# Attention scores in wider visits: from 20 steps of four PSUM banks to 12 visits of six

## The chip, the cores and the metric

The kernel runs on one core of one Trainium2 chip. A core has a matrix engine (TensorE; PE in the profile, PEld for its weight loads), a vector engine (VectorE; DVE), an activation engine (ScalarE; ACT), GpSimd (POOL) and a queue that starts transfers (SyncE; SP). Matrix products land in PSUM, which has eight banks of 512 float32 columns by 128 partitions; everything else works in SBUF. The metric is the device time of one execution in microseconds (us), the median of three runs, lower is better.

## The reference, cut to what matters

32 images of 256 channels by 1024 positions (S) pass a group norm, three 1x1 projections to queries, keys and values, and strictly causal attention with 8 heads of 32 channels; the input is added to the result. All is float32.

```python
q = einsum('oc,bcs->bos', q_w, gn(x)) + q_b          # and kv likewise; 8 heads of 32
mask = tril(ones((S, S)), -1)                        # key strictly before query
scores = where(mask == 0, -10000, q @ k^T / sqrt(32))
attn = where(mask == 0, 0, softmax(scores))
x = x + attn @ v
```

The kernel computes the exponentials without subtracting a maximum, sums them, and multiplies the result by the inverse sums. A slower path that subtracts the maximum stands behind a range check of the sums and isn't entered here.

## The kernel before, in words

**Tiling.** Scores are held transposed: 128 keys on the partitions, queries along the columns. A head has 32 channels, so a product of one head's keys and queries uses 32 of the 128 rows of the matrix array, and four heads (one of two groups `g`) are multiplied side by side, each on its own quarter of the rows and into its own PSUM bank. The queries of an image come in two halves `hf` of 512 columns; keys come in eight blocks `k` of 128. Blocks wholly hidden by the mask are not computed, and the short ends are packed: half 0 takes three steps, half 1 seven. Per image that is 2 x (3 + 7) = 20 steps, 12 of them 512 columns a head, 4 of them 384 + 128 columns (two key blocks in one step), 4 of them 256 columns.

**A step** (`scores`, line 243) takes two PSUM tiles of two banks each out of a pool of three (`ps_s`, six banks), multiplies the four heads into them (line 252; tile `sT` in the profile), lets ACT take the exponential of each tile into SBUF (line 259; tile `e`), and has POOL zero the masked corner (line 265). Two steps later (`LAG = 2`) `values` (line 273) multiplies those exponentials with the values of the four heads, side by side on four quarters of the array's columns, into one bank (`acc`, line 283), and DVE adds the exponentials into the running sum (line 288). Behind the last step of a half ACT copies `acc` out (`num`, line 292). `sums` (line 295) adds over the keys with a product of ones (`pd`, line 301), copied out by ACT (`den`, line 306).

**The projections** of the next image fill in between: twelve units per image, eight of 512 columns (`pp`, tiles `q` and `k`) and four for the values (`ppv`, tile `v`), each one bank of products (line 146) and one ACT copy (line 208 or 224). They, `pd` and the norm's tiny products (`pm`, `pv`) share one PSUM bank, `misc`. Six banks of `ps_s`, one of `acc` and one of `misc` make all eight.

**The order** on PE, ACT, DVE and POOL is written out by hand: at step `i` the scores of step `i`, then the functions entered for `i` in the table `at` (projections, norm, finishing), then the values of step `i - 2`, then the table `after` (the sums). The offsets are in `PROJECT`, `PREPARE`, `SUMS` and `FINISH` (lines 387 to 390). Each engine works through its list in order and waits for semaphores that the framework sets. The finished sums go through DRAM: SP writes `den` out, `gather` reads all four back as one tile, DVE inverts it, SP writes the inverse and reads it back spread over the partitions (`rb`), and DVE multiplies, adds the bias and `x` (`finish`, lines 346 and 347).

Of the kernel before, what the change touches and what calls it, by code (L numbers as in the profile page):

```python
# [17 lines left out]
P = 128  # L18
HD = 32
# [6 lines left out]
SUM_MAX = 1.0e20  # L26
ROW = 64
LAG = 2
# [3 lines left out]
def tile_norm_attention_residual(  # L32
# [83 lines left out]
    def unshifted():  # L116
        live = {}
        xpool = tc.alloc_tile_pool(name="xpool", bufs=4)
# [10 lines left out]
        qkpool = tc.alloc_tile_pool(name="qkpool", bufs=4)  # L129
        epool = tc.alloc_tile_pool(name="epool", bufs=4)  # L130
# [104 lines left out]
        def blocks(hf, k):  # L235

            d = k - hf * BPH
            own = slice(max(d, 0) * P, HALF)
            if d == 1:
                return [(k, own, own), (k + 2, slice(0, P), slice(HALF - P, HALF))]  # L240
            return [(k, own, own)]

        def scores(b, g, hf, k):
            q, kk = live["q", b, g], live["k", b, g]
            d = k - hf * BPH
            tag = "e0" if k == 0 else "e"
            e = epool.tile([P, 4, HALF], F32, tag=tag, bufs=3 if k == 0 else None, name=f"{tag}_{b}_{g}_{hf}_{k}")
            pairs = [ps_s.tile([P, 2, HALF], F32, tag="sT", name=f"sT_{b}_{g}_{hf}_{k}_{a}") for a in range(2)]
            for kb, cols, of in blocks(hf, k):
                for j in range(4):  # L250
                    rows = slice(HD * j, HD * (j + 1))
                    nc.tensor.matmul(  # L252
                        pairs[j // 2][:, j % 2, cols], lhsT=kk[rows, kb * P : (kb + 1) * P],
                        rhs=q[rows, hf * HALF + of.start : hf * HALF + of.stop],
                        start=True, stop=True, skip_group_check=True,
                    )
            c0 = 2 * P if d == 2 else 0
            for a in range(2):
                nc.scalar.activation(e[:, 2 * a : 2 * a + 2, c0:], pairs[a][:, :, c0:], AF.Exp)  # L259
            if d >= 0:  # L260


                n = 2 if d == 1 else 1
                diagonal = e[:, :, c0 : c0 + n * P].rearrange("p j (n q) -> p j n q", q=P)
                nc.gpsimd.affine_select(  # L265
                    out=diagonal, in_=diagonal, pattern=[[0, 4], [0, n], [1, P]],
                    compare_op=ALU.is_gt, fill=0.0, base=0, channel_multiplier=-1,
                )
                if k == 0:
                    nc.gpsimd.memset(e[0:1, :, 0:1], 1.0)  # L270
            live["e", b, g, hf, k] = e

        def values(b, g, hf, k):
            last = k == hf * BPH + 2
            e = live.pop(("e", b, g, hf, k))
            if k == 0:
# [3 lines left out]
            for kb, cols, of in blocks(hf, k):  # L280
                for j in range(4):
                    h = 4 * g + j
                    nc.tensor.matmul(  # L283
                        acc[HD * j : HD * (j + 1), of], lhsT=live["v", b][:, kb, h * HD : (h + 1) * HD],
                        rhs=e[:, j, cols], start=k == 0, stop=last, skip_group_check=True,
                    )
                if k:
                    nc.vector.tensor_add(total[:, :, of], total[:, :, of], e[:, :, cols])  # L288
            if last:
                if (g, hf) == (0, 0):  # L290
                    live["num", b] = work.tile([P, NG, S], F32, tag="num", name=f"num_{b}")
                nc.scalar.copy(live["num", b][:, g, hf * HALF : (hf + 1) * HALF], acc)  # L292
# [72 lines left out]
        per = [(g, hf, k) for g in range(NG) for hf in range(NH) for k in range(hf * BPH + 3)]  # L365
        steps = [(b, *s) for b in range(B) for s in per]
        N = len(per)
# [5 lines left out]
        def prepare(b, whens):  # L373
            both = [slice(hf * HALF, (hf + 1) * HALF) for hf in range(NH)]
            for n, f in zip(whens, (
# [4 lines left out]
                if n is None:  # L380
                    f()
                else:
                    when(n, f)
# [3 lines left out]
        PROJECT = (-6, -5, -3, -2, -1, 1, 4, 5, 7, 8, 9, 11)  # L387
        PREPARE = (-36, -35, -30, -28, -20, -19, -18, -18)
        SUMS = LAG + 2
        FINISH = (N + 11, N + 12, N + 14, N + 15)  # L390
        every = range(4)

        with tc.manual_schedule(engines={ENG.PE, ENG.Activation, ENG.DVE, ENG.Pool}):
            prepare(0, [None] * 8)
            for n, f in zip((None, None, 0, 0, 1, 1) + PROJECT[6:], projections(0)):
                if n is None:
                    f()
                else:
                    when(n, f)
            if B > 1:  # L400
                prepare(1, (None, None, 2, 4, 6, 7, 8, 9))
            for b in range(B):
# [4 lines left out]
                if b >= 2:  # L407
                    when(max(first - 2 * N - 2, 0), lambda b=b: load(b))
                    prepare(b, [first + n for n in PREPARE])
                for s, (g, hf, k) in enumerate(per):  # L410
                    if k == hf * BPH + 2:
                        n = first + s + (LAG if last and s == N - 1 else SUMS)
                        when(n, lambda b=b, g=g, hf=hf: sums(b, g, hf), after)
                if not last:
                    when(first + N + 4, lambda b=b: gather(b, every))
                    when(first + N + 6, lambda b=b: check_sums(b, every))
                    when(first + N + 6, lambda b=b: invert(b, every))
                    for n in every:
                        when(first + FINISH[n], lambda b=b, n=n: finish(b, n))
                else:  # L420
                    when(first + N - 4, lambda b=b: gather(b, every[:3]), after)
                    when(first + N - 2, lambda b=b: check_sums(b, every[:3]))
                    when(first + N - 2, lambda b=b: invert(b, every[:3]))
                    for n in every[:3]:
                        when(first + N + n - 1, lambda b=b, n=n: finish(b, n))
                    when(first + N + LAG, lambda b=b: gather(b, every[3:]))
                    when(first + N + LAG, lambda b=b: finish_last(b))
                    when(first + N + LAG, lambda b=b: check_sums(b, every[3:]))
            for i in range(max(max(at), max(after), len(steps) + LAG) + 1):
                if i < len(steps):  # L430
                    scores(*steps[i])
                for f in at.get(i, ()):
                    f()
                if LAG <= i < len(steps) + LAG:
                    values(*steps[i - LAG])
                for f in after.get(i, ()):
                    f()

# [6 lines left out]
        for p in reversed(pools):  # L445
            p.release()
        return outside
# [149 lines left out]
```

## Time and profile before

| | us |
|---|---|
| median of three runs | 2073.38 (2070.18 to 2073.43) |
| the profiled execution's own time | 2069.36 |
| its span in the trace | 2067.4 |
| PE busy | 2009.1 (97%) |
| ACT busy | 1501.4 (73%) |
| DVE busy | 1474.5 (71%) |
| POOL busy | 449.8 (22%) |

The granted TensorE clock is 0.994 of full speed over the span. A row of the profile names the line of the kernel, the engine, the operation, the tile written and those read, and the shape; a product in float32 leaves two MATMUL records, since the engine goes over it in two passes. The ends of MATMUL records are modelled, so the distance from one row's start to the next row's start says more than the length of a row.

### The profile page before, as it was taken

To read this page: it belongs to the slowest core of one execution; us is meant where nothing else is said; L and a number is where in the kernel's file an instruction comes from. 1 tells how busy PE (TensorE), PEld (TensorE's weight loads), DVE (VectorE), ACT (ScalarE), POOL (GpSimd) and SP (SyncE) were. 2 spreads that over 40 slices of the span, in tenths; PEclk is the share of its full clock that TensorE was granted. 3 is DMA by queue.
4 is the path that set the end of the run, shared out by engine and by line. 5 is a ranking of instruction groups with operands and counts; after the bars stand their busy time and mean duration, and the time that the engine had idled before them with its cause. 6 is when DMAs were issued, how large, how long until landed. Compare 5 with 4: busy or idle time off the path is not lost.

```text
span 2067.4 us, 50451 instructions
## 1 busy us (share of the span) xinstructions
PE 2009.1 (97%) x22030; PEld 712.0 (34%) x22030; DVE 1474.5 (71%) x1480; ACT 1501.4 (73%) x1991; POOL 449.8 (22%) x495
## 2 busy tenths in 40 slices
PE   7999999999999999999999999999999999999994
PEld 2333333333333333333333333333333333333331
DVE  3677777677777777776777777777767777777666
ACT  4777777777777777777777777777777777777773
POOL 1321221212212212212122122122122121222221
PEclk9999999999999999999999999999999999999997
DMA  2011011111111110111111111111111101111101
GB/s 100 2 64 64 34 54 44 63 64 45 50 48 52 63 65 33 55 46 61 64 56 42 48 50 64 64 36 52 49 58 65 64 34 51 47 64 44 39 34 54
DMA packets 56782, 107.76 MB, mean 52 GB/s; under 512 B 14188, under 2 KB 15340, under 8 KB 56556
## 3 DMA queue, kind: packets, MB, share of 16 engines
q1 hardware_dynamic: 54780, 103.56, 14.2%
q8 instruction: 174, 2.85, 0.6%
q10 hardware_dynamic: 1776, 0.92, 0.2%
q14 instruction: 52, 0.43, 0.1%
HBM read 68.82 MB, written 35.64 MB: 51 GB/s over the span
## 4 chain that ended last, share of the span: by engine, by line
PE 87%; ACT 4%; issue 4%; POOL 3%; DVE 1%; DMA 1%; ACTq 0%; POOLq 0%; SPq 0%; DVEq 0%
PE sT L252 27%; PE pp L146 23%; PE acc L283 23%; PE ppv L146 9%; PE pd L301 5%; POOL e L265 3%; ACT e L259 2%; ACT num L292 1%; ACT k L208 1%; DMA qk_bias<-in_L_conv_q_b_dram 0%; PE pm L146 0%; DVE e L288 0%; DMA rb<-inverses 0%; DVE rb L359 0%; DVE rb L347 0%
## 5 line engine op out<-in xcount | busy, mean ns | idle before, releaser
L259 ACT ACTIVATE e<-sT 128x1024 f32<-128x1024 f32 (+1 forms) x1280 | 1132.5, 937 | 461.1 <-PE sT L252 454.2
L288 DVE TENSOR_TENSOR e<-e,e 128x2048 f32<-128x2048 f32 (+3 forms) x640 | 1086.1, 1697 | 377.3 <-PE acc L283 258.7
L265 POOL TENSOR_SCALAR_AFFINE_SELECT e<-e 128x512 f32<-128x512 f32 (+1 forms) x384 | 420.5, 1095 | 1575.5 <-ACT e L259 1465.1
L252 PE MATMUL sT<-q,k 32*128 32x512 f32 (+3 forms) x6144 | 684.0, 524 | 0.8 <-ACT k L208 0.8
L283 PE MATMUL acc<-e,v 128*32 128x512 f32 (+3 forms) x6144 | 617.4, 489 | 18.8 <-ACT num L292 10.0
L146 PE MATMUL pp<-xn,wT 128*32 128x512 f32 x4096 | 493.7, 600 | 2.4 <-ACT q L208 0.9
L252 PEld LDWEIGHTS sT<-q,k 32*128 32x128 f32 x6144 | 273.1, 183 | 458.9 <-issue 384.0
L283 PEld LDWEIGHTS acc<-e,v 128*32 128x32 f32 x6144 | 175.1, 110 | 366.3 <-issue 232.8
L146 PE MATMUL ppv<-wT,xn 128*32 128x256 f32 x4096 | 247.6, 382 | 0.8 <-ACT k L208 0.8
L146 PEld LDWEIGHTS pp<-xn,wT 128*32 128x32 f32 x4096 | 107.1, 109 | 282.6 <-issue 174.1
L191 DVE TENSOR_SCALAR xn<-x,mean,rstd 128x512 f32<-128x512 f32 x128 | 73.0, 630 | 175.1 <-POOL rstd L184 175.1
L146 PEld LDWEIGHTS ppv<-wT,xn 128*32 128x32 f32 x4096 | 120.0, 109 | 123.8 <-ACT den L306 47.0
L301 PE MATMUL pd<-e,pick 128*32 128x512 f32 x1024 | 134.2, 596 | 13.3 <-DVE e L288 12.2
L208 ACT ACTIVATE q<-pp,qk_bias 128x512 f32<-128x512 f32 x128 | 88.1, 689 | 31.5 <-PE pp L146 31.5
L208 ACT ACTIVATE k<-pp,qk_bias 128x512 f32<-128x512 f32 x128 | 88.1, 688 | 28.7 <-PE pp L146 26.9
L347 DVE SCALAR_TENSOR_TENSOR rb<-rb,v_bias_col,x 128x512 f32<-128x512 f32 x129 | 105.6, 819 | 4.6
L346 DVE TENSOR_TENSOR rb<-num,rb 128x512 f32<-128x512 f32 x129 | 87.6, 679 | 4.3 <-DMA rb<-inverses 4.3
L306 ACT COPY den<-pd 128x512 f32<-128x512 f32 x128 | 75.0, 586 | 14.7 <-PE pd L301 14.7
L156 DVE BATCH_NORM_STATS2 st<-x 128x6 f32<-128x512 f32 x128 | 81.9, 681 | 5.2 <-DMA x<-in_x_dram 5.2
L224 ACT COPY v<-ppv 128x512 f32<-128x512 f32 x128 | 75.1, 586 | 4.2 <-PE ppv L146 2.1
L292 ACT COPY num<-acc 128x512 f32<-128x512 f32 x128 | 74.8, 585 | 3.9 <-PE acc L283 3.9
L301 PEld LDWEIGHTS pd<-e,pick 128*32 128x32 f32 x1024 | 31.8, 110 | 52.4 <-issue 37.7
(40 smaller groups left out, 153.5 us busy)
## 6 DMA issues: line engine op xcount, KB each, us to landing
x<-in_x_dram SPq DMA_DIRECT2D x64, 512.0 KB
rb<-inverses SPq DMA_DIRECT2D x127, 256.0 KB
out_dram<-rb SPq DMA_DIRECT2D x127, 256.0 KB
sums<-den SPq DMA_DIRECT2D x128, 8.0 KB
rows<-sums SPq DMA_DIRECT2D x31, 32.0 KB
inverses<-inv SPq DMA_DIRECT2D x31, 32.0 KB
wn<-in_L_conv_kv_w_dram ACTq DMA_DIRECT2D x2, 256.0 KB
wn<-in_L_conv_q_w_dram ACTq DMA_DIRECT2D x1, 256.0 KB
```

Of the source, the lines that this page charges most:

```text
L146: nc.tensor.matmul(out[part], lhsT=lhsT[:, part], rhs=rhs, start=start, stop=stop, skip_group_check=True)
L156: nc.vector.bn_stats(st[:, c, :], live["x", b][:, g, c * HALF : (c + 1) * HALF])
L208: nc.scalar.activation(live[key][:, cols], pp, AF.Identity, bias=qk_bias[:, n, g : g + 1], scale=(SCALE, 1.0)[n],)
L252: nc.tensor.matmul(pairs[j // 2][:, j % 2, cols], lhsT=kk[rows, kb * P : (kb + 1) * P], rhs=q[rows, hf * HALF + of.start : hf * HALF + of. ...
L259: nc.scalar.activation(e[:, 2 * a : 2 * a + 2, c0:], pairs[a][:, :, c0:], AF.Exp)
L265: nc.gpsimd.affine_select(out=diagonal, in_=diagonal, pattern=[[0, 4], [0, n], [1, P]], compare_op=ALU.is_gt, fill=0.0, base=0, channel_mu ...
L283: nc.tensor.matmul(acc[HD * j : HD * (j + 1), of], lhsT=live["v", b][:, kb, h * HD : (h + 1) * HD], rhs=e[:, j, cols], start=k == 0, stop= ...
L288: nc.vector.tensor_add(total[:, :, of], total[:, :, of], e[:, :, cols])
L292: nc.scalar.copy(live["num", b][:, g, hf * HALF : (hf + 1) * HALF], acc)
L301: nc.tensor.matmul(pd[HD * j : HD * (j + 1), :], lhsT=pick, rhs=total[:, j, :], start=True, stop=True, skip_group_check=True,)
L346: nc.vector.tensor_mul(rb[:, g, cols], num[:, g, cols], rb[:, g, cols])
L347: nc.vector.scalar_tensor_tensor(rb[:, g, cols], rb[:, g, cols], v_bias_col[:, g : g + 1], xt[:, g, cols], ALU.add, ALU.add)
```

## The change

A **visit** takes the place of a step. It holds a full piece (up to 512 columns for each of the four heads, in four banks) and a half piece (256 columns for each head, in two banks), and takes all three tiles of `ps_s` at once: six banks. There are 6 visits for a group of heads, 12 for an image. To have as many half pieces as full ones, key blocks 1 and 2 of half 1 are cut into two pieces of 256 columns each; the two 256-column ends of before are the other two half pieces. Columns in total stay as they were.

The half piece has four heads and two banks. Heads 2 and 3 are multiplied first, into the upper halves of banks 4 and 5; then the full piece, heads 0 to 3 into banks 0 to 3; then heads 0 and 1 into the lower halves of banks 4 and 5. The first two products raise a semaphore of their own (`bank_free`), on which TensorE waits before the last two. ACT takes three exponentials of 1024 elements (line 302 twice, line 303), where it took two.

The values lag by one visit, not two steps. The projections stand one at each visit. `values` of a half-cut block are two products of 256 columns with two additions on DVE. The tables of offsets are rewritten, and `prepare` and `finish` go into `after`, behind the values of their visit. Pools shrink: `qkpool` 4 to 3, `epool` 4 to 3, with a tag `eh` of 4 half-wide buffers. At the end of the last image the three first finishes stand behind all additions on DVE, and not between them.

On PE, before, in the second half of an image's first group of heads (`sT_0_1_3` are the scores of group 0, half 1, key block 3; `pp_1_0_0` is a projection unit; `pd_0` the first sum):

```order
L252 MATMUL sT_0_1_2_0_2144<-q_0_1830,k_0_1859 128x512 x2
L252 MATMUL sT_0_1_2_1_2145<-q_0_1830,k_0_1859 128x512 x2
L146 MATMUL pp_1_0_0_2153<-xn_1477,wT 32x512 x8
L283 MATMUL acc_0_1_2167<-e_3_0_1_0_2075,v_1907 32x512 x4
L252 MATMUL sT_0_1_3_0_2173<-q_0_1830,k_0_1859 128x512 x2
L252 MATMUL sT_0_1_3_1_2174<-q_0_1830,k_0_1859 128x512 x2
L283 MATMUL acc_0_1_2167<-e_0_1_1_2102,v_1907 32x512 x4
L301 MATMUL pd_0_2197<-e_3_0_0_0_1988,pick 32x512 x4
```

And now, the visit of the same key block:

```order
L255 MATMUL sT_0_1_3_2_2285<-q_0_1944,k_0_1988 128x256 x2
L255 MATMUL sT_0_1_3_0_2283<-q_0_1944,k_0_1988 128x512 x2
L255 MATMUL sT_0_1_3_1_2284<-q_0_1944,k_0_1988 128x512 x2
L255 MATMUL sT_0_1_3_2_2285<-q_0_1944,k_0_1988 128x256 x2
L147 MATMUL pp_1_0_0_2299<-xn_1590,wT 32x512 x8
L325 MATMUL acc_0_1_2309<-e_3_0_1_0_2227,v_2043 32x512 x4
L325 MATMUL acc_0_1_2309<-eh_0_0_1_2165,v_2043 32x256 x4
L325 MATMUL acc_0_1_2309<-eh_0_1_0_2228,v_2043 32x256 x4
L343 MATMUL pd_0_2324<-e_3_0_0_0_2118,pick 32x512 x4
```

Two runs of scores with values behind each have become one run of scores, one of projections, and one of values with the sum behind it.

On PE around the second unit of the value projection (`ppv_1`, key blocks 2 and 3), before; the values that read it first are those of `e_0_0_2`, three steps later and out of this piece:

```order
L146 MATMUL ppv_1_854<-wT,xn_509 32x256 x16
L283 MATMUL acc_1_1_694<-e_1_1_6_787,v_731 32x256 x4
L252 MATMUL sT_0_0_2_0_880<-q_0_657,k_0_683 128x256 x2
L252 MATMUL sT_0_0_2_1_881<-q_0_657,k_0_683 128x256 x2
L283 MATMUL acc_0_0_894<-e_1_0_0_0_812,v_731 32x512 x4
```

And now; `eh_0_0_0` holds key block 2, which needs `ppv_1`:

```order
L255 MATMUL sT_0_0_1_2_2168<-q_0_1944,k_0_1988 128x256 x2
L147 MATMUL ppv_1_2186<-wT,xn_1590 32x256 x16
L325 MATMUL acc_0_0_2204<-e_3_0_0_0_2118,v_2043 32x512 x4
L325 MATMUL acc_0_0_2204<-eh_0_0_0_2119,v_2043 32x256 x4
L343 MATMUL pd_3_2214<-e_2_1_1_0_1927,pick 32x512 x4
```

The products that read that projection have come to stand one product behind it.

On ACT, before (`den_0` is the copy of `pd_0`):

```order
L259 ACTIVATE e_0_1_2_1555<-sT_0_1_2_0_1556 128x1024
L259 ACTIVATE e_0_1_2_1555<-sT_0_1_2_1_1557 128x1024
L208 ACTIVATE q_1_1564<-pp_1_0_0_1565,qk_bias 128x512
L259 ACTIVATE e_0_1_3_1584<-sT_0_1_3_0_1585 128x1024
L259 ACTIVATE e_0_1_3_1584<-sT_0_1_3_1_1586 128x1024
L306 COPY den_0_1614<-pd_0_1609 128x512
```

And now:

```order
L302 ACTIVATE e_0_1_3_1649<-sT_0_1_3_0_1651 128x1024
L302 ACTIVATE e_0_1_3_1649<-sT_0_1_3_1_1652 128x1024
L303 ACTIVATE eh_0_1_3_1650<-sT_0_1_3_2_1653 128x2x2x256
L209 ACTIVATE q_1_1666<-pp_1_0_0_1667,qk_bias 128x512
L348 COPY den_0_1697<-pd_0_1692 128x512
```

The copy of a projection stands behind three exponentials of its visit, not two. The diff, cut to its core:

```diff
-        qkpool = tc.alloc_tile_pool(name="qkpool", bufs=4)
-        epool = tc.alloc_tile_pool(name="epool", bufs=4)
+        qkpool = tc.alloc_tile_pool(name="qkpool", bufs=3)
+        epool = tc.alloc_tile_pool(name="epool", bufs=3)
...
+        def scores(b, full, half):
...
+            e = epool.tile([P, 4, HALF], F32, tag=tag, name=f"{tag}_{name}")
+            eh = epool.tile([P, 4, HALFBANK], F32, tag="eh", bufs=4, name=f"eh_{name}")
+            pairs = [ps_s.tile([P, 2, HALF], F32, tag="sT", name=f"sT_{name}_{a}") for a in range(3)]
+            short = pairs[2].rearrange("p bank (n q) -> p bank n q", n=2)
+            first = [scores_of((b, half), short[:, j % 2, 1, :], j, name) for j in (2, 3)]
+            for j in range(4):
+                scores_of((b, full), pairs[j // 2][:, j % 2, :], j, name)
+
+            for ins in first:
+                ins.then_inc(bank_free, 1)
...
+            live["free"] = live.get("free", 0) + len(first)
+            wait = nc.tensor.wait_ge(bank_free, live["free"])
...
+            for j in range(2):
+                lo = scores_of((b, half), short[:, j, 0, :], j, name)
...
+            for a in range(2):
+                nc.scalar.activation(e[:, 2 * a : 2 * a + 2, :], pairs[a], AF.Exp)
+            exp = nc.scalar.activation(eh.rearrange("p (n bank) q -> p bank n q", n=2), short, AF.Exp)
...
+            mask(full, e)
+            mask(half, eh)
...
+            visits += [
+                (f[0][0], f[0][2]), (f[0][1], h[1, 0]), (f[1][0], h[1, 1]),
+                (f[1][3], h[2, 0]), (f[1][4], h[2, 1]), (f[1][5], f[1][6]),
+            ]
+            products += [
+                (f[0][0], f[0][2]), (f[0][1],), (f[1][0], h[1, 0], h[1, 1]),
+                (f[1][3], h[2, 0]), (f[1][4], h[2, 1]), (f[1][5], f[1][6]),
+            ]
...
-        PROJECT = (-6, -5, -3, -2, -1, 1, 4, 5, 7, 8, 9, 11)
-        PREPARE = (-36, -35, -30, -28, -20, -19, -18, -18)
-        SUMS = LAG + 2
-        FINISH = (N + 11, N + 12, N + 14, N + 15)
+        PROJECT = (-4, -3, -2, -1, 0, 1, 2, 3, 4, 5, 6, 7)
+        PREPARE = (-22, -21, -20, -19, -18, -16, -11, -11)
+        SUMS = (3, 7, 9, 13)
+        FINISH = (N + 7, N + 7, N + 8, N + 9)
...
-            for i in range(max(max(at), max(after), len(steps) + LAG) + 1):
-                if i < len(steps):
-                    scores(*steps[i])
-                for f in at.get(i, ()):
+            for i in range(B * N + 1):
+                if i < B * N:
+                    scores(i // N, *visits[i % N])
+                for f in at.pop(i, ()):
                     f()
-                if LAG <= i < len(steps) + LAG:
-                    values(*steps[i - LAG])
-                for f in after.get(i, ()):
+                if i:
+                    for pc in products[(i - 1) % N]:
+                        values((i - 1) // N, pc)
+                for f in after.pop(i, ()):
                     f()
```

In `visits` and `products`, `f[hf][k]` is the full piece of key block `k`, and `h[k, n]` the n-th 256 columns of a cut block.

More of the change, by code (lines that the diff above doesn't have):

```diff
@@ L230, in projections, with piece @@
             return qk[0] + v[:1] + qk[1] + v[1:3] + qk[2] + v[3:] + qk[3]
-        def blocks(hf, k):
+        def piece(g, hf, k, part=None):
             d = k - hf * BPH
-            own = slice(max(d, 0) * P, HALF)
             if d == 1:
[L240 to L257, printed above, removed]
-            for a in range(2):
[L259 to L271, printed above, removed]
@@ L426, in unshifted @@
[L426 to L436 removed]
+                        when(first + N, lambda b=b, n=n: finish(b, n), after)
@@ L446, in unshifted @@
             p.release()
+        for ins in nc.cur_bb.bb.instructions:
+            if "TilePoolBoundary op=release" in ins.concise():
+                tc.declare_no_dep(ins, group="first", reason="exponentials behind them are waited for")
         return outside
```

104 lines of the change are left out of this document (77 added, 27 removed).

## The prediction

> **What bounds the kernel now.** First the page: span, busy time and the chain that ended last.
>
> ```profile
> span 2067.4 us, 50451 instructions
> PE 2009.1 (97%) x22030; PEld 712.0 (34%) x22030; DVE 1474.5 (71%) x1480; ACT 1501.4 (73%) x1991; POOL 449.8 (22%) x495
> PE 87%; ACT 4%; issue 4%; POOL 3%; DVE 1%; DMA 1%; ACTq 0%; POOLq 0%; SPq 0%; DVEq 0%
> ```
>
> TensorE sets the end, so the question is what its time is made of. The chain in order of time shows the same product once an image:
>
> ```profile
> 124.99 1.90 PE pp L146 x16
> ...
> 1763.68 1.90 PE pp L146 x16
> ```
>
> These lie 26 images apart: 1638.69 / 26 = 63.03 us an image. 32 images are 2017; the other 50 us are head and tail. Next, PE's own rows in the middle of an image; I read distances from start to start.
>
> ```profile
> 1020.68 1.04 PE L283 MATMUL acc<-e,v 128*32 128x512 f32 x8
> 1021.65 1.14 PE L252 MATMUL sT<-q,k 32*128 32x512 f32 x8
> 1022.72 1.06 PE L283 MATMUL acc<-e,v 128*32 128x512 f32 x8
> 1023.61 1.04 PE L301 MATMUL pd<-e,pick 128*32 128x512 f32 x8
> 1024.58 1.14 PE L252 MATMUL sT<-q,k 32*128 32x512 f32 x8
> 1025.65 1.93 PE L146 MATMUL ppv<-wT,xn 128*32 128x256 f32 x32
> 1027.40 1.04 PE L283 MATMUL acc<-e,v 128*32 128x512 f32 x8
> 1028.37 1.15 PE L252 MATMUL sT<-q,k 32*128 32x384 f32 x16
> 1029.45 1.92 PE L146 MATMUL pp<-xn,wT 128*32 128x512 f32 x16
> 1031.19 1.04 PE L283 MATMUL acc<-e,v 128*32 128x512 f32 x8
> 1032.16 0.71 PE L252 MATMUL sT<-q,k 32*128 32x256 f32 x8
> 1032.81 1.50 PE L146 MATMUL pp<-xn,wT 128*32 128x512 f32 x12
> ```
>
> Scores of 512 columns take 1.07 (1024.58 to 1025.65), of 256 columns 0.65: 0.42 for 256 columns, both passes, four heads abreast. `pp` runs 1024 columns in 1.74, at most 0.00170 a column. I use 0.00167, 0.43 per 256. What is left is fixed: 1.07 - 0.85 = **0.22** for going into scores and out again, whatever their width (0.65 - 0.43 is 0.22 too). Values of 512 columns take 0.89 with `pd` behind them and 0.97 with scores behind them (both 0.85 by columns), so the way into scores adds 0.12. Every run of scores costs **0.34** beyond its columns, 20 times an image, 6.8 of 63.
>
> **The change, part by part.**
>
> *Fewer runs of scores.* 12 instead of 20: 8 x 0.34 = -2.72 an image. Columns stay: 9216 of scores and as many of values. Cutting values into 256-column products costs nothing by the rows: two products in one run follow each other without a gap (384 + 128 in a run of scores took 1.08, against 1.07 in one piece). I add 0.01 a visit.
>
> *Inside the visit.* Before no run mixes heads of different lengths. The new one takes 768 columns a head, 1.28 + 0.22 = 1.50, if heads 2 and 3 (256, then 512) run beside heads 0 and 1 (512, then 256). Bounds: nothing added; or, if one of the two overlaps fails, 256 columns more, +0.43. The nearest row is the eight passes of four heads in 1.07: two passes for each head, four heads abreast, so a head's second pass in the queue doesn't hold up the next head's first. I take 0.
>
> *The added wait.* It stands in front of heads 0 and 1 of the half piece; behind it in PE's queue are those, the projection and the values. It is satisfied when the first two products end, 0.1 (half of the 0.22, taken as the way in) + 0.43 after the visit's start, plus a signal. An exponential follows the end of its scores by about 0.2 us (scores start at 1024.58, their columns end about 1025.54, ACT starts at 1025.75, below). That gives 0.74; heads 0 and 1 are busy with the full piece until 0.96. Nothing queued misses the wait: cost 0, with 0.2 in reserve. Without that cover, every 0.1 us is 384 x 0.1 = 38 us.
>
> *All six banks.* The next visit's first products need the third exponential done. ACT's rows:
>
> ```profile
> 1024.71 0.59 ACT L306 COPY den<-pd 128x512 f32<-128x512 f32 x1
> 1025.75 1.94 ACT L259 ACTIVATE e<-sT 128x1024 f32<-128x1024 f32 x2 [0.45 <-PE sT L252]
> 1027.65 0.59 ACT L224 COPY v<-ppv 128x512 f32<-128x512 f32 x1
> 1029.55 1.94 ACT L259 ACTIVATE e<-sT 128x1024 f32<-128x1024 f32 x2 [1.32 <-PE sT L252]
> 1031.44 0.69 ACT L208 ACTIVATE q<-pp,qk_bias 128x512 f32<-128x512 f32 x1
> ```
>
> And the groups of exponentials, masks and additions (busy us in total, mean ns of one, then the idle time ahead of them by what ended it):
>
> ```profile
> L259 ACT ACTIVATE e<-sT 128x1024 f32<-128x1024 f32 x1024 | 993.1, 1022 | 408.7 <-PE sT L252 401.8 <-DVE rb L347 0.8 <-issue 0.7
> L265 POOL TENSOR_SCALAR_AFFINE_SELECT e<-e 128x1024 f32<-128x1024 f32 x128 | 151.6, 1184 | 214.5 <-ACT e L259 213.5 <-DVE dev L171 1.0
> L288 DVE TENSOR_TENSOR e<-e,e 128x2048 f32<-128x2048 f32 x256 | 586.7, 2292 | 195.4 <-PE acc L283 146.8 <-POOL e L265 35.6
> L288 DVE TENSOR_TENSOR e<-e,e 128x1024 f32<-128x1024 f32 x128 | 154.9, 1210 | 3.6
> ```
>
> The first exponential starts 1.17 after its scores (1024.58 to 1025.75); two take 1.94, one 1.02, so they follow each other every 0.92. The third ends 1.17 + 0.92 + 0.92 + 1.02 = 4.03 after the visit's start. The shortest visit on PE (third and ninth of an image) is 1.50 + 1.75 + 0.85 + 0.12 = 4.22. The wait is covered, by 0.19; the other visits take 4.6 to 6.
>
> *Copies behind the exponentials.* A projection's copy now starts at 1.17 + 3 x 0.92 = 3.93 and ends at 4.52 (`v`) or 4.62 (`q`, `k`). In the second visit the values of key block 2 need `ppv_1` of that visit; PE is there at 1.50 + 1.75 + 0.85 = 4.10: a new wait of 0.45 to 0.5. In three visits (`pm`, `pv`, `pd_1`) the single `misc` bank is wanted at 1.50 + 1.74 + 1.28 = 4.52 and free at about 4.67: 0.13 to 0.15 each. Together +0.9 an image.
>
> *Waits that go.* Twice an image values waited for the copy of the bank before them, and some scores for a tile of `ps_s`:
>
> ```profile
> 1009.57 0.71 PE L252 MATMUL sT<-q,k 32*128 32x256 f32 x8
> 1010.59 1.06 PE L283 MATMUL acc<-e,v 128*32 128x512 f32 x8 [0.30 <-ACT num L292]
> ```
>
> 1.02 where 0.65 would do, so 2 x 0.37. Now a projection stands between. For the tiles I take 0.2 an image: -0.9 in all.
>
> *DVE and POOL.* Four whole additions an image become eight halves: 4 x (2 x 1.210 - 2.292) = +0.5 us of DVE, which has this load over ten images (the window and its length, then busy us of PE, PEld, DVE, ACT and POOL, the granted clock, the share of the transfer engines, GB/s):
>
> ```profile
> 100.00:730.30 630.30, 625.22 (x6884) 221.60 (x6880) 458.88 (x461) 468.01 (x621) 138.93 (x150) 1.00 0.15 53
> ```
>
> 46.4 of 60.5 an image: hidden. Were it not, sums come late and `pd` waits. Masks (1.18 and 1.05 to 1.2) end 5.4 after a visit's start, and values read them at 4.22 + 3.25 at the earliest: hidden by the visit between.
>
> *An image:* 12 x (1.50 + 1.745 + 0.12) = 40.4; values 9216 x 0.00167 = 15.4; four `pd` at 0.88, 3.5; norm products 0.3; new waits 0.9; total 60.5. From the other side: 63.03 - 2.72 - 0.9 + 0.9 + 0.1 = 60.4. That is -2.55 x 32 = **-82 us**.
>
> *Tail.* In the last image DVE stalls and finishes ahead of the additions that the last sum needs:
>
> ```profile
> 2042.28 0.69 DVE L346 TENSOR_TENSOR rb<-num,rb 128x512 f32<-128x512 f32 x1 [4.26 <-DMA rb<-inverses]
> ...
> 2051.42 1.22 DVE L288 TENSOR_TENSOR e<-e,e 128x1024 f32<-128x1024 f32 x1
> 2055.31 1.76 DVE L359 RECIPROCAL rb<-pd 128x256 f32<-128x256 f32 x1 [2.67 <-ACT den L306]
> ```
>
> Now the additions come first, and `pd` and its copy (2051.42 to 2055.31, 3.9 with the last addition) lie beside three finishes (3 x 1.5): -9 from the stall and that overlap. Against it, the last four visits have no projections and are paced by ACT's 4.03 instead of 3.0: +4. The transfers for `rb` start some 2 us earlier or later, as DVE comes to the inverse: I take **-5**, between -10 and +3. The head stays within 2.
>
> **Sum.** 2069.4 - 82 - 5 = 1982 for an execution like the profiled one; the median of the runs lies 4.0 above that one. Predicted: **1987** us, 4.2% less.
>
> **Rivals.**
>
> *Row quarters take turns (slower).* If PE starts the full piece of heads 0 and 1 only when the half pieces in front of it have ended, each visit has 1024 columns in series: 384 x 0.43 = +164, so 2151. It decides from (2073 - 1987) / 384 = 0.22 us a visit. Against it: the 1.07 for eight passes. For it: a head's products now differ in length from its neighbours', and no row shows that. The Trainium skill, "TensorE: Matmul & The Clock Gate", Part 3 ("The mechanism"), says that matmuls start and end strictly in program order and only weight loads are pulled ahead. By that rule, applied to passes, one head's second pass would hold up the next head; the row of 1.07 (it would be 5 x 0.43 = 2.1) speaks against it here. Chance 0.09.
>
> *A late signal or a late ACT.* If `bank_free` comes 0.1 us beyond its reserve, +38; if the first exponential starts only behind the whole visit's scores (1.50 + 0.2 instead of 1.17), the third ends at 4.56, and two visits gain 0.4 and four waits 0.5 each: 2.8 an image, +90. For it: reserves of 0.2 everywhere. Against: the first two heads' columns end at 0.96, and the semaphore counts in PE's order, full piece of heads 0 and 1 first. 2015 to 2069, chance 0.20.
>
> *The gain is real but hidden anyway* (DVE or the `rb` transfers set the pace): within 0.2%, chance 0.04. At 77% of DVE and 15% of the transfer engines little speaks for it.
>
> *Better than forecast,* if the new waits are absent (0.9 x 32 = 29): below 1965, chance 0.02.
>
> **How the numbers follow.** The forecast, 1965 to 2015, has 0.65. To leave out no more than 2 in 10 the range takes in a part of the late-signal case, to 2035, and not the slower rival: 1965 to 2035. About 0.2% is what a measurement of this kernel can tell from no change. Faster 0.65 + 0.20 + 0.02 = 0.87, same 0.04, slower 0.09.
>
> **What would show it.** Right: the image's period near 60.5; a row of scores followed by a projection 1.50 after its start; 0.4 to 0.5 of wait in front of `eh`'s values on ACT's `v`; no wait of scores on ACT over 0.2. Wrong: scores of 1.9 us (the slower rival), `sT` waiting for ACT in every visit (ACT's pace), or `pd` waiting for DVE.

## The result, and the profile after

| | before | after |
|---|---|---|
| median of four runs, us | 2072.78 (2070.18 to 2073.43) | 1991.24 (1989.97 to 1993.09) |
| the profiled execution's own time | 2069.36 | 1992.32 |
| its span | 2067.4 | 1990.4 |

With a fourth run the median of before is 2072.78 in place of 2073.38. The ratio is 0.961, with a 95% interval of 0.9593 to 0.9626. The forecast was 1987, in a range of 1965 to 2035.

The page of the changed kernel, with the same three lines as before:

```profile
span 1990.4 us, 54612 instructions
PE 1941.6 (98%) x24078; PEld 961.9 (48%) x24078; DVE 1559.4 (78%) x1608; ACT 1462.8 (73%) x1863; POOL 580.1 (29%) x495
PE 91%; ACT 5%; issue 2%; DVE 1%; DMA 1%; ACTq 0%; POOL 0%; SPq 0%; DVEq 0%
```

TensorE still sets the end, on 91% of the chain. In the chain of waits in order of time, the same projection of two images:

```profile
55.50 1.86 PE ppv L147 x32
...
1753.05 1.86 PE ppv L147 x32
```

They lie 28 images apart: 1697.55 / 28 = 60.63 us an image, where it was 63.03 and 60.5 was forecast. 32 x 2.40 is 77, and the span fell by 77.0: nearly all of the gain is in the period. PE's rows in the middle of an image (start, length, then line, tile and shape; what counts is the distance between starts):

```profile
1002.73 1.67 PE L255 MATMUL sT<-q,k 32*128 32x256 f32 x24
1004.33 1.93 PE L147 MATMUL ppv<-wT,xn 128*32 128x256 f32 x32
1006.08 1.04 PE L325 MATMUL acc<-e,v 128*32 128x512 f32 x8
1007.42 0.64 PE L325 MATMUL acc<-eh,v 128*32 128x256 f32 x8 [0.30 <-ACT v L225]
1007.85 1.07 PE L343 MATMUL pd<-e,pick 128*32 128x512 f32 x8
1008.85 1.57 PE L255 MATMUL sT<-q,k 32*128 32x256 f32 x16
1010.35 1.93 PE L147 MATMUL ppv<-wT,xn 128*32 128x256 f32 x32
1012.10 1.05 PE L325 MATMUL acc<-e,v 128*32 128x384 f32 x16
1013.08 1.57 PE L255 MATMUL sT<-q,k 32*128 32x256 f32 x16
1014.58 1.92 PE L147 MATMUL pp<-xn,wT 128*32 128x512 f32 x16
...
1023.12 0.61 PE L325 MATMUL acc<-eh,v 128*32 128x256 f32 x8
1023.69 0.24 PE L147 MATMUL pm<-mv,avg 128*32 128x2 f32 x8
1023.86 1.67 PE L255 MATMUL sT<-q,k 32*128 32x256 f32 x24
...
1037.66 0.61 PE L325 MATMUL acc<-eh,v 128*32 128x256 f32 x8
1038.15 1.06 PE L343 MATMUL pd<-e,pick 128*32 128x512 f32 x8
```

An ordinary visit's scores take 1.50 (1008.85 to 1010.35; 1013.08 to 1014.58), as forecast. A visit whose full piece has two key blocks (384 and 128 columns, so 24 records in place of 16) takes 1.60 (1002.73 to 1004.33), which was not forecast. Values of 512 columns with `eh` behind them take 1.34 (1006.08 to 1007.42) where 0.86 would do: 0.48, the forecast wait for `v`. ACT's rows of the first of these visits:

```profile
1003.95 1.94 ACT L302 ACTIVATE e<-sT 128x1024 f32<-128x1024 f32 x2 [0.49 <-PE sT L255]
1005.77 1.03 ACT L303 ACTIVATE eh<-sT 128x1024 f32<-128x1024 f32 x1
1006.67 0.60 ACT L225 COPY v<-ppv 128x512 f32<-128x512 f32 x1
```

The copy ends at 1007.27, 4.54 after the visit's start (4.52 forecast), and the values that need it start at 1007.42.

### The profile page after: what moved, and what is told of

Same layout as the page of the kernel before. It is cut to its first block, busy times and chain, and to the rows that moved or that the text cites. A ratio compares the mean times of both kernels' runs of the same rounds, so it can differ in the third digit from the quotient of the medians.

```text
span 1990.4 us, 54612 instructions
## 1 busy us (share of the span) xinstructions
PE 1941.6 (98%) x24078; PEld 961.9 (48%) x24078; DVE 1559.4 (78%) x1608; ACT 1462.8 (73%) x1863; POOL 580.1 (29%) x495
## 4 chain that ended last, share of the span: by engine, by line
PE 91%; ACT 5%; issue 2%; DVE 1%; DMA 1%; ACTq 0%; POOL 0%; SPq 0%; DVEq 0%
PE sT L255 29%; PE pp L147 24%; PE acc L325 23%; PE ppv L147 9%; PE pd L343 6%; ACT e L302 3%; ACT v L225 1%; ACT eh L303 1%; DMA rb<-inverses 0%; DVE e L330 0%; DMA qk_bias<-in_L_conv_q_b_dram 0%; PE pm L147 0%; PE pv L147 0%; DVE rb L389 0%; DVE rb L388 0%
## 5 line engine op out<-in xcount | busy, mean ns | idle before, releaser
L302 ACT ACTIVATE e<-sT 128x1024 f32<-128x1024 f32 x768 | 744.9, 1022 | 278.5 <-PE sT L255 232.4
L330 DVE TENSOR_TENSOR e<-e,eh 128x1024 f32<-128x1024 f32 x384 | 543.8, 1430 | 384.0 <-PE acc L325 363.4
L330 DVE TENSOR_TENSOR e<-e,e 128x1536 f32<-128x1536 f32 (+2 forms) x384 | 638.2, 1662 | 17.3 <-POOL e L270 2.0
L255 PE MATMUL sT<-q,k 32*128 32x256 f32 (+3 forms) x7168 | 618.1, 460 | 0.8 <-ACT k L209 0.8
L255 PEld LDWEIGHTS sT<-q,k 32*128 32x128 f32 x7168 | 463.3, 184 | 203.6 <-issue 106.7
L325 PE MATMUL acc<-e,v 128*32 128x512 f32 (+2 forms) x4096 | 400.7, 486 | 0.9 <-POOL e L270 0.9
L303 ACT ACTIVATE eh<-sT 128x1024 f32<-128x1024 f32 x384 | 396.0, 1031 | 0.0
L325 PE MATMUL acc<-eh,v 128*32 128x256 f32 x3072 | 225.1, 380 | 9.5 <-ACT v L225 9.5
L325 PEld LDWEIGHTS acc<-eh,v 128*32 128x32 f32 x3072 | 96.2, 110 | 182.6 <-issue 134.0
L270 POOL TENSOR_SCALAR_AFFINE_SELECT eh<-eh 128x512 f32<-128x512 f32 x128 | 164.1, 1282 | 2.6
```

The source lines that it names most:

```text
L255: ins = nc.tensor.matmul(pair[:, cols], lhsT=live["k", b, g][rows, kb * P : (kb + 1) * P], rhs=live["q", b, g][rows, hf * HALF + of.start ...
L270: nc.gpsimd.affine_select(out=diagonal, in_=diagonal, pattern=[[0, 4], [0, n], [1, P]], compare_op=ALU.is_gt, fill=0.0, base=0, channel_mu ...
L302: nc.scalar.activation(e[:, 2 * a : 2 * a + 2, :], pairs[a], AF.Exp)
L303: exp = nc.scalar.activation(eh.rearrange("p (n bank) q -> p bank n q", n=2), short, AF.Exp)
L325: nc.tensor.matmul(acc[HD * j : HD * (j + 1), of], lhsT=live["v", b][:, kb, h * HD : (h + 1) * HD], rhs=e[:, j, cols], start=first, stop=l ...
```

## The experiments

The changed kernel is called "the change" below. Periods are us an image, read from start to start of `pd`.

**1. What a run of scores costs.** A score product of two columns stands ahead of the values of half 1; the values overwrite what it writes.

```diff
+            if first and hf == 1:
+                nc.tensor.matmul(
+                    acc[:, 0:2], lhsT=live["k", b, g][0:HD, 0:P], rhs=live["q", b, g][0:HD, 0:2],
+                    start=True, stop=True, skip_group_check=True,
+                )
```

> The changed kernel with one tiny score product (32 rows, 2 columns) ahead of the first values product of each half 1: 64 more runs of score products with almost no columns in them. Theory (a run of scores costs 0.34 us beyond its columns, 0.22 going in and out and 0.12 on the way in): 64 x 0.34 = +22 us, up to +28 where the small run also ends the overlap of a neighbour (0.1 each). Rival (what a run costs lies in its waits and its width, not in the change between score and value products): 64 x 0.002, so under 2 us.

Measured: 2020.64, 29.4 more than the change. PE's rows of this kernel:

```profile
999.55 1.92 PE L147 MATMUL pp<-xn,wT 128*32 128x512 f32 x16
1001.40 0.38 PE L323 MATMUL acc<-q,k 32*128 32x2 f32 x2
1001.71 1.06 PE L330 MATMUL acc<-e,v 128*32 128x512 f32 x8
```

`pp` with values behind it takes 1.74 without the tiny product (1029.45 to 1031.19 in the prediction's rows). Here it is 1.85 to the tiny product and 0.31 more to the values: 0.42. The period rose by 0.89 for two of them, 0.445 each. The rival (under 2 us) falls. The forecast of 22 to 28 is a little low: 0.11 stands ahead of the tiny product (0.12 forecast), and 0.33 comes behind its start, where 0.22 was forecast. The other 0.11 is probably the tiny product's own two loads and passes; no run separates it. A small product as such is cheap: the eight records of `pm` are two columns wide too, but split the array as the values do, and they take 0.17 with scores behind them (1023.69 to 1023.86 in the change), of which 0.12 is the way into the scores. So the price lies in the change of kind: scores use 32 rows by 128 columns of the array (32\*128 in the rows), values and projections 128 by 32. The Trainium skill ("TensorEngine Tiling (Array Packing)", "Key Properties") says that changing the tiling mode drains the engine, and gives no price. The cost in these rows fits that and gives its size here; the draining itself they do not show.

**2. Do the row quarters run on their own?** The half pieces no longer lie beside the full piece of the other heads.

```diff
-            first = [scores_of((b, half), short[:, j % 2, 1, :], j, name) for j in (2, 3)]
             for j in range(4):
                 scores_of((b, full), pairs[j // 2][:, j % 2, :], j, name)
+            first = [scores_of((b, half), short[:, j % 2, 1, :], j, name) for j in (2, 3)]
...
```

> The changed kernel with the half pieces no longer beside the full piece of the opposite heads: first the full piece of all four heads, then the half piece of heads 2 and 3, then, behind the same semaphore, that of heads 0 and 1. Theory (the four row quarters run on their own, so the order of the changed kernel has 768 columns in series and this one has 512 + 256 + 256 with two waits for a signal of 0.25): a run of scores takes about 2.3 us in place of 1.50, 384 x 0.78 = +300 us; at the very least one piece of 256 more, 384 x 0.43 = +164. Rival (quarters take turns already in the changed kernel): 384 x 0.25 for the second signal at most, and scores that take the same columns, so under +100 us.

Measured: 2257.76, 266 more than the change and a ratio of 1.0895 (1.0875 to 1.0915) to before. PE's rows:

```profile
1109.82 2.37 PE L255 MATMUL sT<-q,k 32*128 32x512 f32 x16
1112.11 1.92 PE L147 MATMUL pp<-xn,wT 128*32 128x512 f32 x16
...
1141.99 1.04 PE L324 MATMUL acc<-e,v 128*32 128x512 f32 x8
1142.97 0.64 PE L324 MATMUL acc<-eh,v 128*32 128x256 f32 x8
```

The scores take 2.29 (2.3 expected): the same products in another order cost 0.79 a visit more. Of that 0.43 is a piece of 256 columns that no longer lies beside another, and 0.36 the signal and the weight load behind it, during which TensorE has nothing else to do. So in the change the quarters do run beside each other; without that the 0.43 alone, 384 x 0.43 = 165 us by estimate, would have made it slower than before. The rise is 266 and not 300 for two reasons. The copies come earlier against the longer visits: `v` makes 0.98 (1141.99 to 1142.97) of what was 1.34, and the waits of `pm`, `pv` and `pd` go, 0.77 an image together. And a visit with two key blocks takes 2.32 in place of 1.60, 0.72 more. 8 x 0.79 + 4 x 0.72 - 0.77 is 8.43, and the period rose by 8.47.

**3. More runs in the kernel before.** Key blocks 1 and 2 of half 1 are cut in two, 24 steps in place of 20.

```diff
-        per = [(g, hf, k) for g in range(NG) for hf in range(NH) for k in range(hf * BPH + 3)]
+        cut = {0: (0, 1, 2), 1: (0, (1, 0), (1, 1), (2, 0), (2, 1), 3, 4, 5, 6)}
+        per = [(g, hf, k) for g in range(NG) for hf in range(NH) for k in cut[hf]]
```

> The kernel before, with key blocks 1 and 2 of half 1 cut into steps of 256 columns: 24 steps an image in place of 20, the same columns, no bank shared by turns. Theory (the gain comes from fewer runs of scores, so more runs lose it again at the same price): 4 x 32 = 128 more runs at 0.34 = +44 us. Rival (what helps is the even length of the visits, or more banks, and a run as such costs nothing): the columns are the same, so within 5 us.

Measured: 2260.13, 188 more than before, a ratio of 1.0907 (1.0891 to 1.0924). Neither number holds. PE's rows:

```profile
1011.88 0.71 PE L257 MATMUL sT_2a<-q,k 32*128 32x256 f32 x8
1012.52 0.64 PE L289 MATMUL acc<-e_1a,v 128*32 128x256 f32 x8
...
1033.22 1.15 PE L257 MATMUL sT<-q,k 32*128 32x256 f32 x8
1035.15 1.07 PE L289 MATMUL acc<-e,v 128*32 128x512 f32 x8 [0.78 <-ACT num L298]
```

Where nothing waits, a run of 256 columns takes the 0.64 that the price gives (1011.88 to 1012.52). But the period rose by 6.15, and four runs at 0.34 are 1.4 of that. The rest is waits: some steps lie closer together than ACT's exponential and copies take, and 1.93 stands where 0.65 would do (1033.22 to 1035.15). The tables of offsets, written for 20 steps, stayed as they were, so the edit changes too much at once to measure the price. It does show that cutting alone, with these offsets, loses far more than the price of four runs.

**4. The 0.1 in visits with two key blocks.** The change issues both blocks of head 0, then both of head 1, and so on. Here the first block of all four heads goes ahead of the second.

```diff
-            for j in range(4):
-                scores_of((b, full), pairs[j // 2][:, j % 2, :], j, name)
+            for block in full[4]:
+                for j in range(4):
+                    scores_of((b, full[:4] + ((block,),)), pairs[j // 2][:, j % 2, :], j, name)
```

> The changed kernel with a full piece that has two key blocks issued block by block (384 columns of all four heads, then 128 of all four), not head by head. Theory (in these four visits an image head 3's first weight load waits behind the other heads' queued loads, and starts at 0.54 us in place of 0.33): their scores take 1.50 in place of 1.60, 4 x 32 x 0.1 = -13 us. Rival (a piece of two blocks costs one more pair of passes for each head wherever it stands): 1.60 stays, within 2 us.

Measured: 1998.40, 7 us slower than the change, not 13 faster. PE's rows, and ACT's of the same visit:

```profile
1005.19 1.58 PE L255 MATMUL sT<-q,k 32*128 32x256 f32 x24
1006.70 1.93 PE L147 MATMUL ppv<-wT,xn 128*32 128x256 f32 x32
1008.45 1.04 PE L326 MATMUL acc<-e,v 128*32 128x512 f32 x8
1010.09 0.64 PE L326 MATMUL acc<-eh,v 128*32 128x256 f32 x8 [0.60 <-ACT v L225]
...
1040.15 0.61 PE L326 MATMUL acc<-eh,v 128*32 128x256 f32 x8
1040.95 1.06 PE L344 MATMUL pd<-e,pick 128*32 128x512 f32 x8 [0.18 <-ACT k L209]
```

```profile
1006.61 1.94 ACT L303 ACTIVATE e<-sT 128x1024 f32<-128x1024 f32 x2 [0.70 <-PE sT L255]
```

The first half came true: by the order alone the scores take 1.51. But the second blocks of heads 0 and 1 now stand behind the first blocks of heads 2 and 3, so the exponential of heads 0 and 1 starts 1.42 after the scores (1005.19 to 1006.61), not 1.22 (1002.73 to 1003.95 in the change). The copies behind it come late: `v` makes 1.64 of what was 1.34, `pd` 0.80 of what was 0.49. Per image that is -4 x 0.09 + 0.30 + 0.31 = +0.25, which is what the period shows (60.88).

**5. The wait for `v`.** The second `v` projection moves one visit earlier, in the place of a `k` projection that is read later.

```diff
-            return qk[0] + v[:1] + qk[1] + v[1:3] + qk[2] + v[3:] + qk[3]
+            return qk[0] + v[:1] + qk[1][:1] + v[1:2] + qk[1][1:] + v[2:3] + qk[2] + v[3:] + qk[3]
...
-            for n, f in zip((None, None, 0, 0, 0, 1) + PROJECT[6:], units[:2] + units[4:5] + units[2:4] + units[5:]):
+            for n, f in zip((None, None, 0, 0, 0, 1) + PROJECT[6:], units):
```

The second place is the list of the first image, which follows the new order.

> The changed kernel with the second v projection one visit earlier, in the place of the k projection that follows it. Theory (in the second visit the values of key block 2 wait 0.48 us for the copy of this v, which stands behind three exponentials on ACT): that wait goes, one of 0.12 for the misc bank may come in its place, 32 x 0.36 to 0.48 = -11 to -15 us. Rival (the wait is covered by something later, or moves to the k projection's reader): within 3 us.

Measured: 1976.67, 14.6 less than the change; the period is 60.20. That is 0.43 of the 0.48: the wait was on the path, and 0.06 of a wait of `pd` for the `misc` bank took its place.

**6. Both edits.**

> Both of the two edits together: two-block pieces issued block by block, and the second v projection one visit earlier. Theory (two independent losses, 0.1 in four visits and 0.48 in one): -24 to -28 us, about 1965. Rival (one covers the other): no more than the larger of the two alone, -15.

Measured: 1985.00. 1991.24 - 14.6 + 7.2 = 1983.8: the two add up, but with the sign that experiment 4 shows for the first. Neither expected number holds, since both counted the block order as a gain.

**7. How much room has the third exponential?** It and its mask go behind the projection's copy on ACT.

```diff
...
-                if i < B * N:
-                    scores(i // N, *visits[i % N])
+                third = scores(i // N, *visits[i % N]) if i < B * N else None
                 for f in at.pop(i, ()):
                     f()
+                if third:
+                    third()
```

> The changed kernel with the third exponential and its mask behind the copy of the visit's projection on ACT, so that the two banks with halves come free later. Theory (the third exponential ends at 4.04 of a shortest visit of 4.23, so 0.2 is all the cover there is): it then ends at about 5.1, visits of 4.2 and 4.6 are stretched to it, +3 to +4 us an image, +100 to +130. Rival (the banks are free long before they are wanted): within 5 us.

Measured: 1996.38, +5.1, so it is about the rival's number. PE's rows around a shortest visit:

```profile
1010.37 1.57 PE L255 MATMUL sT<-q,k 32*128 32x256 f32 x16
...
1014.60 1.97 PE L255 MATMUL sT<-q,k 32*128 32x256 f32 x16
1016.49 1.92 PE L147 MATMUL pp<-xn,wT 128*32 128x512 f32 x16
```

The weight loads (PEld) and the third exponential in the same place:

```profile
1014.59 0.31 PEld L255 LDWEIGHTS sT<-q,k 32*128 32x128 f32 x8 [0.20 <-ACT v L225]
1015.43 0.33 PEld L255 LDWEIGHTS sT<-q,k 32*128 32x128 f32 x8 [0.53 <-ACT eh L310]
```

```profile
1014.35 1.03 ACT L310 ACTIVATE eh<-sT 128x1024 f32<-128x1024 f32 x1
```

The third exponential does end at 5.01 (1015.38), as expected. But the next visit starts at 1014.60 all the same: the half piece of heads 2 and 3 and the full piece of heads 0 and 1 go ahead, and only the full piece of heads 2 and 3 waits. By these rows the tile that a visit begins last has the banks that came free last. So the wait begins at 0.33 of a visit and costs 0.39 and 0.48 in the two visits behind a shortest one and 0.06 in one other, 0.93 an image. Against that the copies come earlier, and the waits for `v` (0.98 here from 1007.96, of 1.34), `pm`, `pv` and `pd` lose 0.77. What is left is +0.17 in the period (60.79). So the small total is two large effects that nearly cancel, and not banks that are free long before they are wanted.

**8. Two heads at a time.** With the `v` projection moved as in 5, both blocks of heads 0 and 1, then both of heads 2 and 3.

```diff
...
-            for j in range(4):
-                scores_of((b, full), pairs[j // 2][:, j % 2, :], j, name)
+            for a in range(2):
+                for block in full[4]:
+                    for j in (2 * a, 2 * a + 1):
+                        scores_of((b, full[:4] + ((block,),)), pairs[a][:, j % 2, :], j, name)
```

> The second v projection one visit earlier, and the two key blocks of a full piece issued two heads at a time: both blocks of heads 0 and 1, then both of heads 2 and 3. Theory (block by block over all four heads shortened the scores to 1.51 but put the second block of heads 0 and 1 behind the first of heads 2 and 3, so the first exponential began at 1.42 in place of 1.22 and the copies behind it came late): scores of 1.50 to 1.52 with the first exponential back at 1.2, so -0.08 to -0.1 in four visits an image against the kernel with the v projection alone (1976.7): about 1965. Rival (a 384-column product whose neighbour has not yet got its second block is what delays ACT, in whatever order): no gain, 1976 to 1985.

Measured: 1969.82, 6.9 less than 5; the period is 60.00. PE's rows, and ACT's:

```profile
1020.56 1.58 PE L255 MATMUL sT<-q,k 32*128 32x256 f32 x24
1022.07 1.92 PE L147 MATMUL pp<-xn,wT 128*32 128x512 f32 x16
...
1024.67 0.61 PE L327 MATMUL acc<-eh,v 128*32 128x256 f32 x8
1025.24 1.07 PE L345 MATMUL pd<-e,pick 128*32 128x512 f32 x8
```

```profile
1021.76 1.94 ACT L304 ACTIVATE e<-sT 128x1024 f32<-128x1024 f32 x2 [0.50 <-PE sT L255]
```

Scores 1.51, first exponential at 1.20: the account of experiment 4 holds, though the forecast of about 1965 was missed by 5. Of 4 x 0.09 = 0.35 an image 0.15 is lost again, since two `pd` now come to the `misc` bank 0.07 sooner and wait for it (0.57 from 1024.67, where 0.43 would do).

**9. The copy first, only in long visits.** In the four visits whose `pm`, `pv` or `pd` waits for `misc`, the third exponential goes behind the copy, on top of 8.

```diff
+        LATE = (1, 4, 6, 7)
...
-                if i < B * N:
-                    scores(i // N, *visits[i % N])
+                third = scores(i // N, *visits[i % N]) if i < B * N else None
+                if third and i % N not in LATE:
+                    third()
                 for f in at.pop(i, ()):
                     f()
+                if third and i % N in LATE:
+                    third()
```

> As the kernel with blocks two heads at a time, and in four visits an image that are 4.8 us and longer (where pm, pv, and two pd wait for the misc bank) the third exponential and its mask behind the projection's copy on ACT. Theory (a late third exponential only holds up the full piece of heads 2 and 3 of the next visit, 0.35 into it; in these visits it ends in time; the copy ends 0.9 earlier): the four waits of 0.13, 0.13, 0.06 and 0.06 go at no cost, 32 x 0.38 = -12 us, about 1953. Rival (every late third exponential costs what the short visits showed, 0.4): +30 us or more.

Measured: 1952.87, 17 less than 8; the ratio to before is 0.9425 (0.9412 to 0.9437). PE's rows:

```profile
1016.88 0.61 PE L330 MATMUL acc<-eh,v 128*32 128x256 f32 x8
1017.31 1.04 PE L348 MATMUL pd<-e,pick 128*32 128x512 f32 x8
```

`pd` comes 0.43 after the values' start where it came 0.57 after, and the other three alike, 0.54 an image; the products behind them take 0.1 less in all and two visits with two key blocks 0.03 more. The period is 59.40, 0.61 less. The 1953 was hit by two misses that cancel: 8 saved 5 less than expected and 9 saved 5 more, since 8 had made two of the waits longer and the products behind the waits lost time too. This kernel is faster than the one before and than the change.

## Why the prediction was right, and where it was not

*Fewer runs, 0.34 each: right.* Eight runs fewer are -2.72 an image. No run takes runs away and leaves the rest; the price stands on experiment 1, which puts a run with almost no columns at 0.445, and on the balance of the period below, which closes.

*Inside the visit, "I take 0": right for the lengths.* 1.50 stands in eight of twelve visits, and experiment 2 shows the loss if it were not so. The records of the visit at 1013.08 of the change (us from its start; records of the trace, not a view; a product leaves two passes) show how it is done:

```
0.002  pass of 256 columns  heads 2 and 3, half piece, first
0.015  pass of 512          heads 0 and 1, full piece, first
0.322  pass of 256          heads 2 and 3, half piece, second
0.537  pass of 512          heads 2 and 3, full piece, first
0.548  pass of 512          heads 0 and 1, full piece, second
0.794  weight load          heads 0 and 1, half piece (0.181 long)
0.967  pass of 512          heads 2 and 3, full piece, second
0.977  pass of 256          heads 0 and 1, half piece, first
1.193  pass of 256          heads 0 and 1, half piece, second
```

Heads 0 and 1 start their first pass before heads 2 and 3 start the second pass of a product that stands ahead of it. The Trainium skill ("TensorE: Matmul & The Clock Gate", Part 3, "The mechanism") says that matmuls start and end strictly in program order; for the two passes of these products the rows don't agree, and the slower rival, which rested on such turns, falls with the 1.50 and experiment 2.

*"I add 0.01 a visit" for two products in one run: wrong for four visits.* It was read from a run of the kernel before, whose loops go block by block (384 + 128 in 1.08). The changed code goes head by head, and such a visit takes 0.10 more, 0.39 an image or 13 us. In the records head 3's first load of the full piece then starts 0.54 after the visit's start; with one block a head it starts at 0.33. Experiments 4 and 8 take the 0.1 away by the order alone, and in their records that load is back at 0.33. In 8 the second blocks of heads 0 and 1 still stand ahead of it, so it is not these that hold it up; whether it is head 2's second block or the number of products ahead is open.

*The added wait: right that it costs nothing, wrong on the reserve.* The forecast had a signal at 0.74, wanted at 0.96, with 0.2 to spare. The load behind the semaphore starts at 0.794, and what it takes had been left out of the sum. That can be read where a pass waits for its load alone: in experiment 2 (the visit at 1109.82) the load behind the semaphore starts at 1.666 and the second pass at 1.988, and a pass of 256 columns takes 0.216 (0.977 to 1.193 here), so the first pass began about 0.11 after the load. By that estimate the product could start at about 0.90 in the change; heads 0 and 1 are free at 0.548 + 0.427 = 0.975. Of the 0.2 in reserve about 0.07 is left.

*All six banks: right that it is covered, wrong on by how much.* The third exponential ends 4.04 after the start of a visit of 4.23, as forecast (1012.89 against 1013.08). The cover is not 0.19 but about 0.5 (0.19 + 0.33), since the banks are wanted only 0.33 into the next visit (experiment 7).

*The copies: right.* Forecast +0.9 an image: 0.48 for `v`, and in front of `misc` 0.14 (1023.12 to 1023.69 is 0.57, where 0.43 would do), 0.13 and 0.06. Experiment 5 shows that the first was on the path, experiment 9 the others.

*The waits that go: right.* Forecast -0.9. In the rows of before, beside the 1.02 shown in the prediction:

```profile
1041.13 0.71 PE L252 MATMUL sT<-q,k 32*128 32x256 f32 x8
1042.06 1.07 PE L283 MATMUL acc<-e,v 128*32 128x512 f32 x8 [0.21 <-POOL e L265]
```

0.93 for 0.65, put down here to POOL's mask and not, as in the prediction, to the copy of the bank; so 0.37 + 0.28, and 0.1 in each of two runs of scores that waited for their banks (1.18 for 1.08). No wait of this kind is left in the change.

*The period.* -2.72 + 0.39 + 0.8 - 0.85 is -2.4, the 2.40 measured. The forecast by differences was -2.6: the visits with two key blocks cost 0.39 where 0.1 stood for all visits, the new waits came out 0.1 smaller, and the waits that go gave 0.05 less.

*The tail: wrong in size, -5 forecast.* From the first `pd` of the last image to the end of the span it was 66.9 and is 63.3; a period is 2.4 of that, so the tail gave 1.2. DVE's rows of the change at the end:

```profile
1962.22 1.13 DVE L367 SCALAR_TENSOR_TENSOR in_range<-rows,in_range 96x64 f32<-96x64 f32 x1
...
1970.62 1.23 DVE L330 TENSOR_TENSOR e<-e,eh 128x1024 f32<-128x1024 f32 x1
...
1973.75 0.69 DVE L388 TENSOR_TENSOR rb<-num,rb 128x512 f32<-128x512 f32 x1 [0.33 <-DMA rb<-inverses]
1976.41 0.69 DVE L388 TENSOR_TENSOR rb<-num,rb 128x512 f32<-128x512 f32 x1 [1.19 <-DMA rb<-inverses]
```

The finishes do lie beside the last `pd`, and the stall of 4.26 is gone. But the additions lag so far that the check of the three sums comes at 1962.22, some 10 us before the last `pd` (2034.93 before, some 18 ahead of it), and the transfers for `rb` are late again, 0.33 and 1.19. This part was not tried by a run of its own, so the cause is read from the rows alone. The head took 1.4 longer, within the 2 that was allowed.

*The median: part luck.* The sum gave 1982 for an execution like the profiled one, and that execution took 1992.32, 10 more: 4.8 by the period, 3.8 by the tail and 1.4 by the head. The forecast then added 4.0, by which the median of before lay above its profiled execution; the median of the change lies 1.1 below its own. These 5 are the scatter of the runs, and they make a miss of 10 look like one of 4.

*The rivals.* The late ACT falls with the first exponential at 1.19 (1008.85 to 1010.04), the hidden gain with 77 us saved. The signal used most of its reserve and did not go beyond it. The new waits came, 0.8 an image, so nothing was better than forecast.

## What to carry to other kernels

A run of products that split the array by rows, among products that split it by columns, costs 0.34 to 0.45 us here beyond its columns, at widths from 2 to 768 columns a head. So the number of runs is a quantity to plan for, as long as heads that use different row quarters run side by side within a run. A price read from one order of issue (two blocks for 0.01) does not carry over when the loops are turned round. When a consumer works on pairs of heads, the order that completes a pair first beat the order by blocks, though both take the matrix engine the same 1.51. A wait that costs nothing should be summed down to the last step before the work, the weight load included, before its reserve is believed.

## What the runs showed of the hardware that was not expected

In the first 25 us some products run at about half speed though the granted clock reads 1.00 there: in the change the second projection takes 3.64 where one takes 1.92 later. In the profiles of before and of experiments 4, 5 and 8 the second takes 1.92 already, and in that of experiment 1 the first scores take 2.94 in place of 1.57. One such projection is worth 1.7 us of the head, more than the 1.4 by which the head of the change is longer; the cause of the half speed is open.

Weight loads are taken ahead of running passes, and of loads issued before them, but not without limit. In a visit of the change with two key blocks (the one at 1002.73) head 2's first load of the full piece starts at 0.324, ahead of those for the second blocks of heads 0 and 1 at 0.444 and 0.457, which stand in front of it; head 3's starts only at 0.542. This delay of 0.2 for one head's load made 0.10 of time, with every row quarter's own columns unchanged.
